# Another order of v, q and k and of the weights' combinations, with p1 written into the second group's PSUM bank, in a graph attention kernel

## The chip, the cores and the metric

The kernel runs on one core of one Trainium2 chip. The metric is the device time of one execution in microseconds (us). All runs of this study on one core were in the fast state, with a mean granted TensorE clock of 0.991 to 0.997; where a median is quoted, it is that of three or four executions of a kernel, with their range. The profile is of one such execution.

## The reference, cut to what matters

Two layers on 32 batches of x (512 nodes by 512 features), with one adjacency matrix for all:

```python
# layer 0: a graph convolution, a residual, a layer norm
mi = einsum('bkd,od->bko', x, Wi);  mj = einsum('bkd,od->bko', x, Wj)
x = layernorm(x + deg * (mi + b) + einsum('ij,bjo->bio', a, mj))
# layer 1: attention of 8 heads under the mask adj, a projection, a residual, a layer norm
q, k, v = x @ Wq.T + bq, x @ Wk.T + bk, x @ Wv.T + bv
x = layernorm(x + softmax(mask(q k^T / 8)) v @ Wo.T + bo)
```

## The kernel before

Each 512x512 product with a weight matrix runs in fp32 on TensorE. It is cut into quarters and done with seven quarter products instead of eight, which land in PSUM, TensorE's output memory. They are numbered: product 1 alone is p1, and p1 belongs to all four quarters of the result; products 1 and 2 make the first quarter; 6, 7 and 4 accumulate in one PSUM bank ("the second group" below), which is read out after each of them, with p1 added, into one of the other three quarters; 5 and 3 accumulate in a third group, without p1, and are added to two of these quarters. I write v2 for v's product 2, and so on. The left factors' combinations are made per batch by GpSimd (`combos`), the weights' once at the start (`combine`), and are then fetched from DRAM through a ring of 12 tiles in the order in which TensorE uses them.

There are two PSUM banks for products, "a" and "b". v and k use "a", q uses "b", and one bank can take its next product only when the last has been read out ("evacuated"). This is the evacuation before:

```python
        if i == 1:
            p1 = OPEN[kind, b, "p1"] = work([P, 2, Q], "p1", 3)
            nc.scalar.copy(p1, pm)
        ...
        if kind in ("l0", "pj"):              # layer 0 and the projection: into y = x
            if i == 1:
                for n, f in ((1, 0), (1, 1), (0, 1)):
                    d = quarter(y, n, f)
                    nc.gpsimd.tensor_tensor(d, d, p1, op=OP.add)
            else:
                nc.vector.tensor_tensor(d, d, pm, op=OP.add)
        elif kind == "v":
            if i == 2:                     nc.scalar.copy(d, pm)
            elif i in (6, 7, 4):           nc.vector.tensor_tensor(d, pm, p1, op=OP.add)
            elif i != 1:                   nc.vector.tensor_tensor(d, d, pm, op=OP.add)
        ...                                  # q and k likewise, with their biases
```

A period handles one batch through v, q and k, while the attention steps of the batch before and the projection of the one before that are laid between the products. The list for one batch n (m = n - 2); `apply` is the layer norm's last step, on ScalarE, `l0_norm` a transpose for v, q, k, `ahead` the split of the next x into two parts for the gather, `z` a piece without TensorE work. Further words used below: the gathers are the adjacency matrix times x on TensorE, the base step is x + deg * b on VectorE, oT is the attention's output from which the projection is made, and the fold takes the bias of v through Wo, once:

```python
        res += [norm[0], norm[1], z(apply, n, 1), pc("v", n, 1, "a"), pc("q", n, 1, "b")]
        ...
        res += [norm[2], norm[3], z(combos, TH, n, h, (1, 2)), pc("v", n, 2, "a"), pc("q", n, 2, "b"),
                pc("k", n, 1, "a"), z(combos, TH, n, h, (3, 4)), z(add_bo, n, 0), z(add_bo, n, 1), pc("k", n, 2, "a")]
        if m >= 0:
            res += [z(apply, m, 0), z(apply, m, 1), z(store, m)]
        for i in ORDER[2:]:                       # 6, 7, 4, 5, 3
            res += [pc("v", n, i, "a"), pc("q", n, i, "b")]
            if i == 5 and n + 1 < B and n > 0:
                res += [z(load_x, n + 1)]
        if n + 1 < B:
            res += [z(ahead, n + 1)]
        # then, in phase_a(n + 1): k's products 6, 7, 4, 5, 3 (bank "a") with the gathers of batch n + 1
```

Of the kernel before, what the change touches and what calls it, by code (L numbers as in the profile page):

```python
# [25 lines left out]
def gnn_attention_kernel(  # L26
# [101 lines left out]
    load_x(0)  # L128
    ident = const.tile([P, P], FT, name="ident")
# [5 lines left out]
    W = {}  # L135
    W["wj"] = load_w(big(), wjT, nc.sync)
    W["wi"] = load_w(big(), wiT, nc.sync)
    W["wv"] = load_w(work([P, NC, D], "v", 2), wvT, nc.sync)
    W["wq"] = load_w(work([P, NC, D], "v", 2), wqT, nc.sync)
# [20 lines left out]
    W["wk"] = load_w(big(), wkT, nc.sync)  # L160
    W["wo"] = load_w(wo, woT, nc.sync)
    load_x(1)
# [28 lines left out]
    ahead(0)  # L191

# [3 lines left out]
    def graph_forms():  # L196
        nc.vector.tensor_tensor(adj_f, adjT, adjR.bitcast(FT), op=OP.not_equal)
        nc.vector.reduce_sum(told[:, B * HP:], adj_f.rearrange("p c i -> p (c i)"), axis=AX.X)
        nc.vector.tensor_scalar(told[:, B * HP:], told[:, B * HP:], 2.0 * SAFE, None, op0=OP.mult)
        nc.vector.tensor_scalar(edge, adjT, 0.0, None, op0=OP.not_equal)  # L200
# [8 lines left out]
    def combine(name, eng):  # L209

        w = W[name]
        a11, a12, a21, a22 = [w[:, 2 * j:2 * j + 2, Q * i:Q * i + Q] for i in range(2) for j in range(2)]
        s1, s2, s3, s4, n22 = [t[:, c].rearrange("p (c i) -> p c i", c=2)
                               for t in [work([P, 2, N], "e", 4) for _ in range(3)] for c in range(2)][:5]
        eng.tensor_tensor(s1, a21, a22, op=OP.add)
        eng.tensor_tensor(s2, s1, a11, op=OP.subtract)
        eng.tensor_tensor(s4, a12, s2, op=OP.subtract)
        eng.tensor_tensor(s3, a11, a21, op=OP.subtract)
        nc.scalar.mul(n22, a22, -1.0)
        for i, t in ((6, s2), (7, s3), (4, n22), (5, s1), (3, s4)):  # L220
            WS[name, i] = dram.tile([P, 2, Q], FT, name=f"{name}_{i}")
            nc.sync.dma_start(WS[name, i], t)
# [8 lines left out]
    def prefetch():  # L231
        while len(TILES) < min(len(KEYS), ring.used + RING):
            t = ring_tile()
            nc.sync.dma_start(t, WS[KEYS[len(TILES)]])
            TILES.append(t)
# [103 lines left out]

    def piece(kind, b, i, bank):  # L340
        g = GROUP[i]
        first = (kind, b, g) not in OPEN
        if first:
            OPEN[kind, b, g] = mm_tile(bank)
        pm = OPEN[kind, b, g]
        terms = []
        for name, (quarters, T) in zip(NAMES[kind], sources(kind, b)):
            a = {1: (0, 0), 2: (1, 0), 3: (1, 1)}.get(i)
            terms.append((take((name, i)), quarters(*a) if a else T[:, {5: 0, 6: 1, 7: 2, 4: 3}[i]]))
        for c in range(2):  # L350
            for n, (w, t) in enumerate(terms):
                for kc in range(2):
                    cut = slice(c * P, (c + 1) * P)
                    lhs, rhs = (w[:, kc, cut], t[:, kc, :]) if kind in "qk" else (t[:, kc, cut], w[:, kc, :])

                    nc.tensor.matmul(pm[:, c * Q:(c + 1) * Q], lhs, rhs, start=first,  # L356
                                     stop=(kc == 1 and n == len(terms) - 1), skip_group_check=True)
                    first = False
        prefetch()
        pm = pm.rearrange("p (c i) -> p c i", c=2)  # L360
        if i == 1:
            p1 = OPEN[kind, b, "p1"] = work([P, 2, Q], "p1", 3)
            nc.scalar.copy(p1, pm)  # L363
        p1 = OPEN[kind, b, "p1"]
        f, n = {1: (0, 0), 2: (0, 0), 6: (0, 1), 3: (0, 1), 4: (1, 0), 7: (1, 1), 5: (1, 1)}[i]
        if kind in ("l0", "pj"):
            y = XT[b]
            if i == 1:
                for n, f in ((1, 0), (1, 1), (0, 1)):
                    d = quarter(y, n, f)  # L370
                    nc.gpsimd.tensor_tensor(d, d, p1, op=OP.add)  # L371
            else:
                d = quarter(y, n, f)
                nc.vector.tensor_tensor(d, d, pm, op=OP.add)  # L374
        elif kind == "v":
            if i == 1:
                V[b] = work([P, NC, D], "v", 2)
            d = quarter(V[b], n, f)
            if i == 2:
                nc.scalar.copy(d, pm)  # L380
            elif i in (6, 7, 4):
                nc.vector.tensor_tensor(d, pm, p1, op=OP.add)
            elif i != 1:
                nc.vector.tensor_tensor(d, d, pm, op=OP.add)
        else:
            T, bias = (QT, bq_c) if kind == "q" else (KT, bk_c)
            if i != 1 and (b, f) not in T:
                T[b, f] = work([P, 2, N], kind, 3)
            if i in (6, 7):
                nc.vector.tensor_tensor(T[b, f][:, :, Q * n:Q * n + Q], pm, p1, op=OP.add)  # L390
            elif i != 1:
                for c in range(2):
                    d = T[b, f][:, c, Q * n:Q * n + Q]
                    bc = bias[:, 2 * f + c:2 * f + c + 1]
                    if i == 2:
                        nc.scalar.activation(d, pm[:, c, :], AF.Identity, bias=bc, scale=1.0)
                    else:
                        o = p1[:, c, :] if i == 4 else d
                        nc.vector.scalar_tensor_tensor(d, pm[:, c, :], bc, o, op0=OP.add, op1=OP.add)
# [75 lines left out]
    def phase_a(n):  # L475

        g = [(TR + GA, l0_gather, n, dc) for dc in range(DC)] if n < B else []
        k = [pc("k", n - 1, i, "a") for i in ORDER[2:]] if n > 0 else []
        res = []
        for i in range(max(len(g), len(k))):  # L480
            res += k[i:i + 1] + g[i:i + 1]
            if n == 0 and i == 3:
                res += [z(graph_forms)]
            if i == (3 if n == 0 else 1) and g:
                res += [z(combos, TX, n, lambda j, m: quarter(XD[n], j, m), (1,)),
                        z(combos, TA, n, lambda j, m: quarter(AX_T[n], j, m), (1,))]
        if g:
            res += [z(combos, TX, n, lambda j, m: quarter(XD[n], j, m), (2,)),
                    z(combos, TA, n, lambda j, m: quarter(AX_T[n], j, m), (2,)),
                    z(base, n, 0),  # L490
                    z(combos, TX, n, lambda j, m: quarter(XD[n], j, m), (3, 4)),
                    z(combos, TA, n, lambda j, m: quarter(AX_T[n], j, m), (3, 4)),
                    z(base, n, 1)]
        return res
# [10 lines left out]
    def phase_b(n):  # L505

        m = n - 2
        if m < 0:
            res = []
            for i, bank in ALONE:  # L510
                if n == 0:
                    res += [z(combine, *f) for f in {6: (("wv", nc.vector),), 2: (("wq", nc.vector),),
                                                     5: (("wk", nc.vector),)}.get(i, ())]
                res.append(pc("l0", n, i, bank))
                if i == 4:
                    res += [z(stats, n, 0)]
            return res + [z(apply, n, 0), z(stats, n, 1)]
        res = []
        for i in ORDER:
# [8 lines left out]
            if i == 4:  # L528
                res.append(z(apply, n, 0))
        return res  # L530

    def phase_c(n):
# [4 lines left out]
        res = [z(fold)] if n == 0 else []  # L537
        res += [norm[0], norm[1], z(apply, n, 1), pc("v", n, 1, "a"), pc("q", n, 1, "b")]
        if m >= 0:
            res += [z(stats, m, 1)]  # L540
        res += [norm[2], norm[3], z(combos, TH, n, h, (1, 2)), pc("v", n, 2, "a"), pc("q", n, 2, "b"),
                pc("k", n, 1, "a"), z(combos, TH, n, h, (3, 4)), z(add_bo, n, 0), z(add_bo, n, 1), pc("k", n, 2, "a")]
        if m >= 0:
            res += [z(apply, m, 0), z(apply, m, 1), z(store, m)]
        for i in ORDER[2:]:
            res += [pc("v", n, i, "a"), pc("q", n, i, "b")]
            if i == 5 and n + 1 < B and n > 0:
                res += [z(load_x, n + 1)]
# [4 lines left out]
    def fold():  # L553

        combine("wo", nc.vector)
        pd = mm_tile("b")
        bv_w = work([P, DC, P], "big", 6)
        for dc in range(DC):
            nc.vector.tensor_scalar(bv_w[:, dc, :], ones, bv_c[:, dc:dc + 1], None, op0=OP.mult)
            nc.tensor.matmul(pd, bv_w[:, dc, :], W["wo"][:, dc, :], start=(dc == 0), stop=(dc == DC - 1))  # L560
# [12 lines left out]
    def last_steps():  # L573
# [5 lines left out]
        return [[z(last_load), p[0], FLUSH] + c, [p[1], p[2]], [p[3], p[4]], [p[5], p[6], z(stats, m, 0), z(stats, m, 1)],  # L579
# [8 lines left out]
    def last_load():  # L588
        W["wo"] = load_w(work([P, NC, D], "xh", 3), woT, nc.sync)

    def last_part(hp, half):
# [6 lines left out]
        for ic in range(2 * half, 2 * half + 2):  # L598
            nc.tensor.matmul(ACC[ic], OT[B - 1, hp // 2][:, hp % 2, ic * P:(ic + 1) * P], W["wo"][:, hp, :],
# [28 lines left out]
    combine("wj", nc.gpsimd)  # L628
    combine("wi", nc.vector)
    prefetch()  # L630

    for f in PERIODS[0]:
        run(f)
# [181 lines left out]
```

## Time and profile before

The time was 4021.6 us (4021.29 to 4022.62). A period is the distance between two equal instructions of neighbouring batches.

| what | value | view |
|---|---|---|
| one period, of 29 undisturbed ones | 122.53 us | chain of waits |
| TensorE busy in it | 120.15 us | stretches |
| VectorE, GpSimd, ScalarE busy in it | 80.4, 57.8, 32.9 us | stretches |
| from the start to the first attention scores | 143.20 us | TensorE's timeline |
| from the start to the base step of batch 2 | 252.91 us | chain of waits |
| from the last base step to the end | 215.24 us | chain of waits |

The waits view of TensorE sums what stood before its instructions over the whole execution: engine and line, what was waited for and where that was made, then us in total, times, and the longest.

```profile
PE mma L356 <- issue: 29.3, 30, 1.0
PE mma L356 <- ACT p L363: 20.9, 31, 0.7
PE mmb L280 <- ACT big L286: 14.8, 2, 14.5
PE mma L356 <- DVE v L382: 9.4, 29, 0.3
PE mmb L356 <- POOL big L325: 8.0, 2, 4.9
```

Entries with 29 to 31 times are per-period waits; entries with one or two belong to the start and the end. L356 is the matmul of all quarter products (L380 in the changed kernel), L363 the copy of p1 (L387).

### The profile page before, as it was taken

The page shows a single profiled execution, that of the slowest core. Times are in us where ns is not written, and L with a number is a line of the kernel's source. Part 1 is how long each engine was busy: PE and PEld are TensorE (multiplying, and loading weights), DVE is VectorE, ACT ScalarE, POOL GpSimd, SP SyncE. Part 2 cuts the span into 40 slices and gives each one's busy share as a digit, 9 for nine tenths or more (in the row PEclk, how much of TensorE's full clock was granted, in tenths as well). Part 3 has the DMA queues.
Part 4 walks back from the last instruction along what each step waited for, and adds up shares of the span by engine and source line. Part 5 has one row for each costly group of instructions (what it writes and reads, how often), then busy time and mean ns, then how long its engine had stood idle before and what let it go on. Part 6 is the DMA issues. An engine that isn't in the chain of part 4 may idle for free.

```text
span 4021.7 us, 47158 instructions
## 1 busy us (share of the span) xinstructions
PE 3876.8 (96%) x17418; PEld 2655.3 (66%) x17418; DVE 2608.9 (65%) x3524; ACT 1059.7 (26%) x1483; POOL 1851.6 (46%) x1866
## 2 busy tenths in 40 slices
PE   6999999999999999999999999999999999999997
PEld 4766666666666666666666666666666666666663
DVE  4466666666666666666666666666666666676666
ACT  1212222222222223222222222232222222222222
POOL 3445445445345454454453454444444534544432
PEclk8999999999999999999999999999999999999998
DMA  7333343333333333333333333333333334333330
GB/s 251 103 99 106 108 121 100 103 108 110 110 115 92 113 108 103 122 100 103 108 113 108 118 89 112 109 107 116 105 98 113 107 110 118 95 106 112 105 107 22
DMA packets 284346, 437.55 MB, mean 109 GB/s; under 512 B 23248, under 2 KB 121040, under 8 KB 284112
## 3 DMA queue, kind: packets, MB, share of 16 engines
q1 hardware_dynamic: 283856, 433.94, 35.9%
q8 instruction: 142, 2.33, 0.2%
q0 software_dynamic: 256, 0.53, 0.1%
q14 instruction: 92, 0.75, 0.1%
HBM read 392.96 MB, written 41.42 MB: 108 GB/s over the span
## 4 chain that ended last, share of the span: by engine, by line
PE 81%; DVE 14%; issue 3%; ACT 1%; POOL 1%; DMA 0%; SPq 0%; POOLq 0%; ACTq 0%; DVEq 0%
PE mma L356 32%; PE mmb L356 17%; PE sc L408 10%; PE ov L430 10%; PE mmb L280 6%; DVE xh L293 5%; DVE rl L443 3%; PE ov L437 2%; DVE es L422 2%; DVE e L413 2%; PE sc L273 1%; PE sc L301 1%; DVE ov L448 1%; ACT big L302 0%; ACT p L363 0%
## 5 line engine op out<-in xcount | busy, mean ns | idle before, releaser
L356 PE MATMUL mma<-ring,big 128*128 128x256 f32 x5288 | 1228.1, 382 | 47.3 <-issue 29.3
L356 PEld LDWEIGHTS mma<-ring,big 128*128 128x128 f32 x5288 | 991.6, 190 | 236.4 <-issue 66.3
L412 ACT ACTIVATE sc<-sc 128x1024 f32<-128x1024 f32 x512 | 492.8, 1006 | 1563.2 <-PE sc L408 1562.1
L413 DVE TENSOR_TENSOR e<-sc,edge 128x1024 f32<-128x1024 f32 x512 | 602.4, 1217 | 355.9 <-ACT sc L412 355.9
L419 POOL TENSOR_TENSOR es<-e 128x1024 f32<-128x1024 f32 x128 | 301.0, 2352 | 778.4 <-PE ov L437 778.4
L325 POOL TENSOR_TENSOR big<-big 128x512 f32<-128x512 f32 x384 | 525.0, 1390 | 236.5 <-DVE big L274 196.8
L408 PE MATMUL sc<-q,k 64*128 64x512 f32 x2048 | 509.7, 616 | 0.2 <-ACT big L302 0.2
L430 PE MATMUL ov<-e,v 128*64 128x512 f32 x2048 | 497.5, 607 | 6.5 <-DVE told L448 6.5
L443 DVE RECIPROCAL rl<-ov 128x128 f32<-128x128 f32 x512 | 458.7, 927 | 5.4 <-PE ov L437 1.6
L356 PE MATMUL mma<-big,ring 128*128 128x256 f32 x1792 | 430.2, 383 | 24.6 <-ACT p L363 20.9
L248 POOL TENSOR_SCALAR mv<-mv 128x1 f32<-128x1 f32 x256 | 79.2, 309 | 774.6 <-DVE mv L247 759.8
L356 PE MATMUL mmb<-big,ring 128*128 128x256 f32 x1792 | 432.6, 384 | 0.0
L356 PEld LDWEIGHTS mmb<-big,ring 128*128 128x128 f32 x1792 | 333.1, 190 | 113.9 <-issue 47.9
L356 PEld LDWEIGHTS mma<-big,ring 128*128 128x128 f32 x1792 | 334.8, 190 | 110.5 <-ACT p L363 33.4
L430 PEld LDWEIGHTS ov<-e,v 128*64 128x64 f32 x2048 | 124.7, 136 | 347.5 <-issue 272.8
L422 DVE TENSOR_TENSOR es<-es,e 128x1024 f32<-128x1024 f32 x256 | 313.5, 1225 | 4.4
L408 PEld LDWEIGHTS sc<-q,k 64*128 64x128 f32 x2048 | 176.5, 186 | 209.4 <-issue 195.8
L371 POOL TENSOR_TENSOR xh<-xh,p 128x512 f32<-128x512 f32 x189 | 235.5, 1274 | 104.5 <-ACT p L363 103.8
L374 DVE TENSOR_TENSOR xh<-xh,mma 128x512 f32<-128x512 f32 x189 | 127.8, 676 | 232.4 <-PE mma L356 232.4
L356 PE MATMUL mmb<-ring,big 128*128 128x256 f32 x1080 | 267.3, 392 | 10.7 <-POOL big L325 8.0
L183 POOL TENSOR_TENSOR xlo<-xh,xhi 128x512 fp32r<-128x512 f32 x128 | 162.6, 1281 | 220.8 <-ACT xhi L182 220.7
L356 PEld LDWEIGHTS mmb<-ring,big 128*128 128x128 f32 x1080 | 203.9, 194 | 90.7 <-POOL big L325 33.1
(109 smaller groups left out, 3667.0 us busy)
## 6 DMA issues: line engine op xcount, KB each, us to landing
ring<-wi SPq DMA_DIRECT2D x160, 256.0 KB, 2.6
ring<-wj SPq DMA_DIRECT2D x160, 256.0 KB, 2.8
ring<-wv SPq DMA_DIRECT2D x160, 256.0 KB, 2.7
ring<-wq SPq DMA_DIRECT2D x160, 256.0 KB, 2.7
ring<-wk SPq DMA_DIRECT2D x160, 256.0 KB, 4.4
ring<-wo SPq DMA_DIRECT2D x155, 256.0 KB, 2.6
xh<-in_x_dram SPq DMA_DIRECT2D x32, 1024.0 KB, 5.5
out_dram<-xh SPq DMA_DIRECT2D x31, 1024.0 KB, 5.1
```

The source lines that it names most:

```text
L280: nc.tensor.matmul(pm, parts[w][:, jc, :], adjR[:, jc, :], start=(w == 0 and jc == 0), stop=(w == 1 and jc == NC - 1))
L293: nc.vector.scalar_tensor_tensor(y, b0_r, deg_c[:, ic:ic + 1], y, op0=OP.mult, op1=OP.add)
L325: nc.gpsimd.tensor_tensor(dst, p, q, op=OP.subtract)
L356: nc.tensor.matmul(pm[:, c * Q:(c + 1) * Q], lhs, rhs, start=first, stop=(kc == 1 and n == len(terms) - 1), skip_group_check=True)
L371: nc.gpsimd.tensor_tensor(d, d, p1, op=OP.add)
L408: nc.tensor.matmul(ps[:, s, :], KT[b, hp // 2][r, hp % 2, kc * P:(kc + 1) * P], QT[b, hp // 2][r, hp % 2, :], start=True, stop=True)
L412: nc.scalar.activation(ps, ps, AF.Exp, scale=QSCALE)
L413: nc.vector.tensor_tensor(e, ps, edge[:, kc:kc + 1, :].to_broadcast([P, 2, N]), op=OP.mult)
L419: nc.gpsimd.tensor_add(ES[hp], E[0], E[1])
L422: nc.vector.tensor_add(ES[hp], ES[hp], E[kc])
L430: nc.tensor.matmul(PV[hp][s * HD:(s + 1) * HD, :], V[b][:, kc, c0:c0 + HD], E[kc][:, s, :], start=(kc == 0), stop=(kc == NC - 1))
L443: nc.vector.reciprocal(rl[:, c], pl[:, c])
```

## The change

Its intent: p1 is no longer added three times by GpSimd or VectorE. ScalarE copies it into the bank of the second group (a "seed"), products 6, 7 and 4 accumulate on top of it without clearing, and ScalarE can evacuate products 6, 7 and 4 of v, q and k with a plain copy or bias. A new order of v, q and k is to give each bank's evacuation another product to hide behind. At the start, the weights' combinations come in two parts, placed between the gathers, and the weights are loaded from ScalarE's queue.

```diff
+    def seed(kind, b, bank):
+        pm = OPEN[kind, b, "Y"] = mm_tile(bank)
+        nc.scalar.copy(pm.rearrange("p (c i) -> p c i", c=2), OPEN[kind, b, "p1"])
 ...
-        if first:
+        if first and g == "Y":
+            seed(kind, b, bank)
+            first = False
+        elif first:
             OPEN[kind, b, g] = mm_tile(bank)
 ...
+        new = i in (2, 6, 7, 4)
         if kind in ("l0", "pj"):
-            if i == 1:
-                for n, f in ((1, 0), (1, 1), (0, 1)):
-                    d = quarter(y, n, f)
-                    nc.gpsimd.tensor_tensor(d, d, p1, op=OP.add)
 ...
+        if i == 2 and (kind == "q" or kind == "l0" and b >= 2 or kind == "pj" and b < B - 2):
+            seed(kind, b, bank)
 ...
-        res += [norm[2], norm[3], z(combos, TH, n, h, (1, 2)), pc("v", n, 2, "a"), pc("q", n, 2, "b"),
-                pc("k", n, 1, "a"), z(combos, TH, n, h, (3, 4)), z(add_bo, n, 0), z(add_bo, n, 1), pc("k", n, 2, "a")]
+        res += [pc("v", n, 2, "a"), norm[2], norm[3], z(combos, TH, n, h, (1, 2)), pc("k", n, 1, "a"),
+                z(combos, TH, n, h, (3, 4)), pc("q", n, 2, "b"), pc("k", n, 2, "a"), z(seed, "v", n, "a")]
 ...
-            res += [pc("v", n, i, "a"), pc("q", n, i, "b")]
+            res += [pc("q", n, i, "b"), pc("v", n, i, "a")]
 ...                                       # the start
-    combine("wj", nc.gpsimd)
-    combine("wi", nc.vector)
-    prefetch()
+            # now in parts, inside phase_a(0): wj on GpSimd (part 1 behind all combos), wi on VectorE;
+            # load_x(1) and prefetch() only in front of the first product of layer 0;
+            # fold (bias of v through wo) no longer ahead of v but at the end of phase_a(1)
```

Cut: the second half of the evacuation (q, k, v), the parts of `combine` and `graph_forms`, the moved `add_bo`, and the renaming of weight halves.

## The prediction

> **What bounds the kernel now.** I read the page's busy shares first, then the stretches view over whole periods, then TensorE's and ScalarE's timelines inside one period. The page:
>
> ```profile
> PE 3876.8 (96%) x17418; PEld 2655.3 (66%) x17418; DVE 2608.9 (65%) x3524; ACT 1059.7 (26%) x1483; POOL 1851.6 (46%) x1866
> PE   6999999999999999999999999999999999999997
> PEclk8999999999999999999999999999999999999998
> ```
>
> TensorE is full but for the first and last fortieth, at full clock. The chain view repeats the base step (L293) every 122.53 us (1110.63, 1233.16, ...), one period per batch. The stretches view, columns span, PE, PEld, DVE, ACT, POOL, clock, DMA share, GB/s:
>
> ```profile
> 0.00:175.00 175.00, 135.95 (x566) 102.95 (x567) 82.61 (x100) 32.43 (x52) 70.43 (x68) 0.90 0.57 191
> 1110.63:1233.16 122.53, 120.15 (x548) 82.65 (x546) 80.43 (x111) 32.87 (x46) 57.77 (x59) 1.00 0.36 108
> 2090.90:2213.43 122.53, 120.15 (x548) 82.65 (x546) 80.42 (x110) 32.87 (x46) 57.78 (x59) 1.00 0.37 108
> ```
>
> A period has 120.15 us of matmuls and only 2.38 idle; the start has 39 us idle in 175. So the change can win in two places: the few waits of a period, times about 30, and once in the start. Work taken from VectorE (80 of 122 us) and GpSimd (58) is worth nothing by itself. TensorE's timeline names the waits of one period:
>
> ```profile
> 1180.54 1.99 PE L356 MATMUL mma<-big,ring 128*128 128x256 f32 x8 [0.68 <-ACT p L363]
> 1183.51 1.97 PE L356 MATMUL mma<-ring,big 128*128 128x256 f32 x8 [0.97 <-issue]
> 1198.41 1.99 PE L356 MATMUL mma<-ring,big 128*128 128x256 f32 x8 [0.32 <-DVE v L382]
> ```
>
> The reader should see that all are bank "a" waiting for its own evacuation: k's product 2 for the copy of p1, v's product 6 for k's evacuation, and a later v. The idle entry understates them, because the modelled end of a matmul overlaps the next. From starts: an undisturbed product of v, q or k takes 1.73 us (1185.31 to 1187.03). k1 started at 1177.97, k2 at 1180.54: 0.84 lost. v6 at 1183.51: 1.24 lost. The last, 1196.20 to 1198.41: 0.48 lost. With 0.43 at the projection that waits for oT and 0.41 after a transpose, a period loses 3.4 us. That is all that a perfect new order could win, 2.8%.
>
> **What the Trainium skill says.** "Perfetto Trace Analysis", Matmuls, says that independent matmul groups should rotate through PSUM banks so that an evacuation overlaps the next group's matmuls. The waits above agree: each sits where two neighbours share bank "a". "PSUM — Partial Sum Buffer", The four PSUM rules, says that ScalarE's writes do not set the bits that decide whether a matmul accumulates, so a written seed is kept only where an earlier matmul left the bit set. Here each seeded bank was written in full by a product or a gather before; I expect right results, and no trace yet shows it. "TensorE: Matmul & The Clock Gate", Part 1, gives a half-rate clock after an idle window of about 3.4 us. The start agrees: after a wait of 14.55 us eight gather matmuls took 2.07 us, later 1.20.
>
> **The change, part by part, in a period.**
>
> Removed: 6 GpSimd additions of p1 to x (L371, 1.27 us each, 7.6 us), and VectorE's p1 additions for v, q, k. Products 6, 7, 4 are now evacuated by ScalarE. Added on ScalarE: five seeds, p1 copied into the bank (like L363's 585 ns: 2.9 us), three v copies (1.76) and six evacuations in pairs (0.84 a pair at 1178.17: 5.0), some 9.7 us. ScalarE goes from 32.9 to about 42.6 us of 122.5. None of it is a bound by busy time; what matters is the order in which ScalarE, an in-order engine, reaches it.
>
> The built order on TensorE is now: v2 right after q1; two transposes; k1(a), q2(b), k2(a), q6(b), v6(a), q7(b), scores, values, v7, q4, v4, q5, v5, q3, scores, values, sums, v3(a), k6(a).
>
> Gain 1: between k1 and k2 stands q2, 1.73 us, and p1's copy needs 0.2 to start and 0.58: the 0.84 goes. Between k2 and v6 stands q6: k2's evacuation (0.2+0.84) and v's seed (0.58) take 1.62, just under 1.73: the 1.24 goes nearly whole.
>
> Loss 1, q7. ScalarE's built order there is: k2's pair, v's seed, **four layer norm applications of the older batch**, q6's pair, v6's copy. Before, the four stood in the same place, but q6 and v6 were then evacuated by VectorE:
>
> ```profile
> 1182.57 0.84 ACT L396 ACTIVATE k<-mma,bk_c 128x256 f32<-128x256 f32 x2 [2.08 <-PE mma L356]
> 1183.30 2.92 ACT L253 ACTIVATE xh<-xh,mv 128x512 f32<-128x512 f32 x4
> ```
>
> Four applications take 2.92 us and already had their inputs when ScalarE reached them. Count from k2's end: pair done at 1.04, seed 1.65, applications 4.6, q6's pair 5.45, q7 may start at 5.55. Without the wait it would start after q6 and v6, at 3.45. **Loss 2.1 us**, so the stretch k1 to q7 gives back what it won (0.84+1.24 = 2.08).
>
> Loss 2, k6. Swapping v and q puts v3(a) right in front of k6(a), and k is not seeded early. Before, q3(b) and an attention step stood between them. Now k6 waits for v3's addition on VectorE (0.2 to start, 0.69), then the seed (0.07, 0.58), then the weight load (0.1 to 0.2): **loss 1.7 us**.
>
> Gain 2: the 0.48 at the late v goes, because ScalarE is free there. Gain 3: k3's addition takes 0.69 instead of a 0.88 pair, which brings the oT chain forward by 0.1 to 0.2.
>
> Seeds that I expect hidden: q's (q2's pair and seed take 1.62 beside k2's 1.73), the projection's (scores or a layer 0 product beside it), and layer 0's (VectorE freed the bank at 1124.33, +0.07+0.58 = 1124.98, and product 6 started at 1125.19 anyway).
>
> Sum per period: -0.84 -1.24 -0.48 -0.1 +2.1 +1.7 = **+1.1 us**; over 30 periods **+34 us**.
>
> **The start.** Before, the combinations' output tiles ran out and blocked ScalarE and with it the second gather:
>
> ```profile
> 36.63 2.07 PE L280 MATMUL mmb<-adjR,xhi 128*128 128x512 f32 x4 [14.55 <-ACT big L286]
> 52.66 6.61 PE L356 MATMUL mmb<-ring,big 128*128 128x256 f32 x16 [3.02 <-POOL big L325]
> 86.69 6.64 PE L560 MATMUL mmb<-xh,big 128*128 128x512 f32 x8 [5.51 <-DVE big L559]
> ```
>
> The change takes that copy off ScalarE and places combinations between gathers, so gathers should end near 28 instead of 46. But the layer 0 tiles are now fetched behind the stores of wj's second part, which GpSimd makes after eight combos of 1.27 us: near 40, plus the issue, x(1)'s 1 MB ahead in the queue and 2.7 us to land: layer 0 starts at 43 to 46, no gain. Its seven products (3.45 each) ran from 46.0 to 81.2, 35 us for 24; with the combos done beforehand I expect some 29, two waits of 0.9 (product 2 on p1's copy, 7 on 6) and a cold start included. Gain 6. The bias fold (L560, about 6.6 us cold with a 5.5 wait) leaves the gap between layer 0 and v and returns later at some 3.5 us; that gap was 13.3 (81.2 to 94.5), and should be some 3.5 (stats, GpSimd chain and apply still have to run): gain 10, minus 3.5 for the fold. From v1 on little else. Sum of the start **-13 to -15**.
>
> The end: the last projection waited 4.94 us for GpSimd combos behind p1 additions (3.7 us) that are gone: -3. The last k products all stand in bank "a", and ScalarE's pair is slower than VectorE's addition: +1. Sum **-2**.
>
> Total: 4021.6 + 34 - 14 - 2 = 4040 us.
>
> **Rivals.** (1) The intended gain: every period wait but transpose and oT goes, ScalarE's order does no harm; 2.56 x 30 = 77 us off, with the start 3930. For it: ScalarE is busy only 26%. Against it: q7's wait on ScalarE stands in the built program, and the applications are ahead of it there. It would need ScalarE to reach q6's pair at once; I see no way. Between the two lies a case in which one of my two losses is smaller than I count. (2) ScalarE's queue becomes worse than counted: seeds also delay the exps, scores wait for their tiles, and each period loses 2 to 3 us: 4070 to 4100. For it: ten more operations in a row, several awaited within 1.7 us. Against it: values use the exps of the step before, an attention step's slack. (3) VectorE or GpSimd as the hidden bound, relieved by 8 to 10%: 4000. Against it: in a period TensorE idles 2.38 us only, and only oT's wait hangs on VectorE's length. (4) The start is hidden or worse, because the weights now queue behind adj on ScalarE's queue: +10.
>
> **Range and chances.** The two losses are sums of durations in the trace; an error of 0.8 us per period in either direction is 24 us, the start is good to 8 us. So 4012 to 4066 for 8 in 10. Two per cent faster is below 3941 and needs rival 1 nearly whole: 0.03. Two per cent slower is above 4102, rival 2 at its worst: 0.03. Within 2%: 0.94.
>
> **What would show it.** In the changed profile: a period of about 123.6 us; TensorE's wait at q7 of 1.7 to 2.1 us, released by ScalarE with four applications just before it; a wait of 1.4 to 1.7 at k6, released by the seed; none left at k2 and v6; GpSimd near 50 us and ScalarE near 42 a period; the first scores near 129 instead of 143.20. I am wrong if the period is below 122.5, which means that one of the two losses is not there, or if waits stand at exps or scores.

## The result, and the profile after

The changed kernel took **4077.28 us** (4075.09 to 4078.05), beside 4022.11 us (4021.29 to 4023.55) for the kernel before in the same rounds: a ratio of 1.0136, 95% interval 1.0118 to 1.0153. Ratios here are the mean of one kernel's runs over that of the other's of the same rounds, so not quite the ratio of the medians. The result is correct. It is slower by 1.4%, and 11 us above the upper end of the predicted range.

TensorE's busy tenths are the same digits as before. First the page's busy times, then the stretches view over one period (columns: span, PE, PEld, DVE, ACT, POOL, clock, DMA share, GB/s):

```profile
PE 3872.5 (95%) x17418; PEld 2647.3 (65%) x17418; DVE 2401.4 (59%) x3049; ACT 1364.5 (33%) x2116; POOL 1628.1 (40%) x1678
```

```profile
1133.08:1257.38 124.30, 120.15 (x546) 82.50 (x546) 74.07 (x95) 42.53 (x66) 50.53 (x53) 1.00 0.35 106
```

ScalarE (42.5) and GpSimd (50.5) are where they were predicted, and TensorE's busy time in a period is the same 120.15 us; only the period has grown, by 1.77 us. So the loss is all waiting. From the chain of waits the difference splits into three parts:

| part | before | after | difference | predicted |
|---|---|---|---|---|
| start, to the base step of batch 2 | 252.91 | 262.96 | +10.1 | -14 |
| 29 periods, 122.53 and 124.30 each | 3553.6 | 3604.7 | +51.2 | +34 (for 30) |
| tail | 215.24 | 207.8 | -7.4 | -2 |
| span of the profiled execution | 4021.7 | 4075.5 | +53.8 | +18 |

TensorE's waits view after shows two new entries with 31 times and a new one of 23 us that came once. The entry for p1's copy is as large as before (21.2 beside 20.9 us), but it now stands at another product, v2 instead of k2:

```profile
PE mmb L380 <- issue: 49.3, 31, 1.6
PE mma L380 <- ACT mma L359: 47.9, 31, 4.2
PE mma L380 <- DMA ring<-in_wiT_dram: 23.3, 1, 23.3
PE mma L380 <- ACT p L387: 21.2, 31, 0.7
PE mmb L588 <- DVE big L587: 7.4, 1, 7.4
```

And TensorE's timeline of the period from 1133.08, cut to the three products with a wait of over 0.5 us (v2, q7, k6):

```profile
1192.29 1.99 PE L380 MATMUL mma<-ring,big 128*128 128x256 f32 x8 [0.68 <-ACT p L387]
...
1210.31 1.97 PE L380 MATMUL mmb<-big,ring 128*128 128x256 f32 x8 [1.61 <-issue]
...
1234.64 1.99 PE L380 MATMUL mma<-big,ring 128*128 128x256 f32 x8 [1.46 <-ACT mma L359]
```

The idle entry in brackets understates a wait, so I count from starts, with 1.73 us for an undisturbed product. q1 started at 1189.71 and v2 at 1192.29: 0.85 lost. v6 at 1206.80, q7 at 1210.31: 1.78 lost. v3 at 1231.19, k6 at 1234.64: 1.72 lost. With 0.43 at the projection that waits for oT and 0.41 behind a transpose, as before, that is 5.19 us a period, against 3.40 before. The difference of 1.79 is the growth of the period (1.77). None of the waits at k2, v6 and the late v is left.

**q7 and k6** came as predicted. ScalarE's timeline around q7, then VectorE's and ScalarE's around k6:

```profile
1206.04 0.59 ACT L359 COPY mma<-p 128x512 f32<-128x512 f32 x1
1206.57 2.92 ACT L269 ACTIVATE xh<-xh,mv 128x512 f32<-128x512 f32 x4
1209.39 0.81 ACT L409 ACTIVATE q<-mmb,bq_c 128x256 f32<-128x256 f32 x2
```

```profile
1233.22 0.69 DVE L401 TENSOR_TENSOR v<-v,mma 128x512 f32<-128x512 f32 x1 [2.10 <-PE mma L380]
1234.00 0.59 ACT L359 COPY mma<-p 128x512 f32<-128x512 f32 x1 [2.06 <-DVE v L401]
```

Four applications of the older batch (2.92 us) stand in front of q6's evacuation at 1209.39, and q7 starts when that ends. At k6, the addition and the seed have nothing beside them.

**v2** was not predicted at all. ScalarE's timeline just before it, after the change and then before it:

```profile
1190.95 0.81 ACT L269 ACTIVATE xh<-xh,mv 128x512 f32<-128x512 f32 x1 [1.92 <-POOL mv L266]
1191.67 0.56 ACT L387 COPY p<-mma 128x512 f32<-128x512 f32 x1
```

```profile
1168.23 0.81 ACT L253 ACTIVATE xh<-xh,mv 128x512 f32<-128x512 f32 x1 [1.92 <-POOL mv L250]
1168.95 0.57 ACT L363 COPY p<-mma 128x512 f32<-128x512 f32 x1
```

The picture is the same in both: p1's copy stands behind the newer batch's application, which waits for GpSimd's statistics. But before, two transposes lay between q1 and v2, as TensorE's timeline of the kernel before shows:

```profile
1167.00 1.89 PE L356 MATMUL mmb<-big,ring 128*128 128x256 f32 x8
1168.73 1.04 PE L301 MATMUL sc<-ident,xh 128*128 128x128 f32 x8
1169.60 1.97 PE L356 MATMUL mma<-ring,big 128*128 128x256 f32 x8
```

There p1's copy ended at 1169.52, and v2 began at 1169.60 without a wait: from q1's start to v2's it was 2.60 us, of which the transposes filled 0.87. Now it is 2.58, v2 comes directly behind q1, and 0.85 of it is idle. The delay was always there; the change took away what TensorE did meanwhile. The Trainium skill ("Perfetto Trace Analysis", Per-engine timelines, Tensor Engine Instruction (MATMUL, LD_WEIGHTS)) says that ScalarE, VectorE and GpSimd are "strict FIFO"; these lines agree, because TensorE had left v1 by 1189.71, where q1 starts, while v1's copy began at 1191.67, behind an application with 1.92 us of idle time in front of it.

**The start.** The timeline of the first 60 us, cut to VectorE's base step, GpSimd's combos, the DMA queue (SPq) and TensorE's first product of layer 0; then the fold:

```profile
34.95 5.75 DVE L309 SCALAR_TENSOR_TENSOR xh<-b_r,deg_c,xh 128x512 f32<-128x512 f32 x4
35.18 11.13 POOL L341 TENSOR_TENSOR big<-big 128x512 f32<-128x512 f32 x6 [1.78 <-DVE big L290]
47.56 0.91 SPq L238 DMA_DIRECT2D wj<-e  x2
49.03 0.57 SPq L250 DMA_DIRECT2D ring<-in_wiT_dram  x1
55.08 6.11 PE L380 MATMUL mma<-ring,big 128*128 128x256 f32 x16 [23.33 <-DMA ring<-in_wiT_dram]
```

```profile
138.62 6.43 DVE L309 SCALAR_TENSOR_TENSOR xh<-b_r,deg_c,xh 128x512 f32<-128x512 f32 x4
145.40 5.31 PE L588 MATMUL mmb<-xh,big 128*128 128x512 f32 x8 [7.42 <-DVE big L587]
```

Layer 0 starts at 55.08 instead of 46.02, because the ring's first tile is issued behind the stores of wj's second part, and that part behind GpSimd's combos. Six of these took 11.13 us, 1.85 us each. I had counted with 1.27. VectorE's base step and further two-input operations ran beside them. The trace of the kernel before already had this: at its start seven combos took 11.83 us, 1.69 each, and in a usual period of both kernels the three combos beside the base step take 1.71 to 1.74 us each, the other twelve 1.25 to 1.29. The Trainium skill ("GPSIMD Engine Reference", 1. Specifications) says that GpSimd shares its SBUF interfaces with VectorE and names contention with VectorE's instructions with two SBUF inputs; these times agree with that, though no run here changed that alone. The long combos, 3.5 us more than at 1.27, are one part of the delay: the gathers ended at 31.75 instead of the predicted 28, GpSimd waited 1.78 us for VectorE in front of the six, and the ring's first tile took 6.01 us from its issue to landing, beside 2.7 in the prediction.

The fold, the other piece, now stands behind batch 1's base step (6.43 us), waits 7.42 us, and then takes 5.31 us at a granted clock of 0.68; e7 below shows it at 3.70 without the wait, at a clock of 1.00. Afterwards the first scores start at 150.64 instead of 143.20. The second period has a further 4.24 us at k6: k's seed stands behind the split of the next x on ScalarE, which waits for x's load. That load takes 5.57 us, as usual, but the attention step that otherwise lies between its issue and k6 is missing there. e9 and e11 test this queue.

### The profile page after: what moved, and what is told of

It is laid out like the page before. It is cut to its first block, busy times and chain, and to the rows that moved or that the text cites. A ratio compares the mean times of both kernels' runs of the same rounds, so it can differ in the third digit from the quotient of the medians.

```text
span 4075.5 us, 46994 instructions
## 1 busy us (share of the span) xinstructions
PE 3872.5 (95%) x17418; PEld 2647.3 (65%) x17418; DVE 2401.4 (59%) x3049; ACT 1364.5 (33%) x2116; POOL 1628.1 (40%) x1678
## 4 chain that ended last, share of the span: by engine, by line
PE 77%; DVE 15%; POOL 3%; ACT 2%; issue 2%; DMA 1%; SPq 0%; ACTq 0%; POOLq 0%; DVEq 0%
PE mma L380 32%; PE mmb L380 16%; PE sc L423 10%; PE ov L445 9%; PE mmb L296 6%; DVE xh L309 5%; DVE e L428 3%; DVE rl L458 3%; PE ov L452 2%; PE sc L289 1%; POOL mv L265 1%; DVE st L262 1%; POOL mv L264 1%; PE sc L317 1%; ACT sc L427 1%
## 5 line engine op out<-in xcount | busy, mean ns | idle before, releaser
L458 DVE RECIPROCAL rl<-ov 128x128 f32<-128x128 f32 x512 | 446.4, 917 | 5.7 <-PE ov L452 1.9
L437 DVE TENSOR_TENSOR es<-es,e 128x1024 f32<-128x1024 f32 x256 | 325.9, 1273 | 4.4
L269 ACT ACTIVATE xh<-xh,mv 128x512 f32<-128x512 f32 x256 | 198.6, 809 | 236.6 <-POOL mv L266 221.1
```

The costliest lines, as they stand in the source:

```text
L269: nc.scalar.activation(y, y, AF.Identity, bias=mv[:, 4:5], scale=mv[:, 3:4])
L437: nc.vector.tensor_add(ES[hp], ES[hp], E[kc])
L458: nc.vector.reciprocal(rl[:, c], pl[:, c])
```

## The experiments

**Theory.** In a period, three operations stand at the wrong place of an in-order queue: the older batch's applications before q6's evacuation (q7), the newer batch's application before p1's copy (v2), and v3 directly before k6. The start has two such places, the ring behind wj's second part and the fold behind the base step. Seeding itself is cheap. **Rival A:** seeding and evacuating on ScalarE is the cost, wherever things stand. **Rival B:** the new order is the cost. All kernels gave correct results and were timed in three rounds.

| run | what | median us (range) | ratio to before (95%) | usual period |
|---|---|---|---|---|
| after | the change | 4077.28 (4075.09 to 4078.05) | 1.0136 (1.0118 to 1.0153) | 124.30 |
| e1 | new order, old evacuation | 4024.35 (4023.53 to 4025.83) | 1.0006 (0.9990 to 1.0023) | 122.44 |
| e9 | old order, seeds | 4038.76 (4034.34 to 4041.00) | 1.0038 (1.0021 to 1.0055) | 122.57 |
| e11 | e9, x loaded earlier | 4026.62 (4022.98 to 4027.42) | 1.0010 (0.9993 to 1.0027) | 122.57 |
| e2 | older applications moved | 4022.38 (4020.52 to 4023.81) | 1.0002 (0.9985 to 1.0018) | 122.45 |
| e3 | p1's copies first | 4050.03 (4049.18 to 4051.14) | 1.0070 (1.0053 to 1.0086) | 123.35 |
| e4 | gather between v3 and k6 | 4028.52 (4027.13 to 4030.28) | 1.0015 (0.9998 to 1.0032) | 122.59 |
| e5 | e2, e3, e4 | 3946.18 (3943.04 to 3947.98) | 0.9812 (0.9796 to 0.9828) | 119.79 |
| e10 | e5 with the old evacuation | 3971.00 (3969.31 to 3974.24) | 0.9873 (0.9857 to 0.9890) | 120.45 |
| e6 | ring and wj early | 4058.64 (4057.10 to 4063.81) | 1.0091 (1.0075 to 1.0108) | 124.31 |
| e7 | fold ahead of base | 4071.61 (4069.35 to 4072.83) | 1.0123 (1.0106 to 1.0140) | 124.31 |
| e8 | e5, e6, e7 | 3918.63 (3917.07 to 3921.64) | 0.9745 (0.9729 to 0.9762) | 119.79 |

### e1: the new order with the old evacuation

The evacuation of the kernel before, p1 added by GpSimd and VectorE, in the changed kernel's order:

```diff
-        if first and g == "Y":
-            seed(kind, b, bank)
-            first = False
-        elif first:
+        if first:
 ...          # and the branches for l0, pj, v, q, k as in the kernel before
-                ... pc("k", n, 2, "a"), z(seed, "v", n, "a")]
+                ... pc("k", n, 2, "a")]
```

> The new order alone: the changed kernel with p1 added by GpSimd and VectorE as in the kernel before, no seeds. My theory (the seeds put ScalarE's queue and a longer chain in front of TensorE, the order alone costs only v2's and k6's wait): the 1.6 us wait at q7 goes, k6's wait shrinks from 1.46 to about 0.9 (VectorE's addition without the seed behind it), v2's 0.68 stays; period 121.8 to 122.3 us, time 4003 to 4015. Rival (the new order is what costs, and the seeds earn something back): period over 124.3, time over 4077.

Measured: 4024.35 us, a little above the 4003 to 4015 expected, and a period of 122.44. TensorE's timeline has v2's wait (0.68) as in the changed kernel, and these two, at a q product and at k6:

```profile
1201.87 1.99 PE L372 MATMUL mmb<-big,ring 128*128 128x256 f32 x8 [0.51 <-DVE q L415]
1214.67 1.99 PE L372 MATMUL mma<-big,ring 128*128 128x256 f32 x8 [0.78 <-DVE v L400]
```

I had not expected the first: a q product waits for VectorE, which still evacuates q here. So the new order alone costs nothing in a usual period (122.44 against 122.53), but it doesn't bring much either. Rival B falls.

### e9: the old order with the seeds

```diff
-        res += [pc("v", n, 2, "a"), norm[2], norm[3], z(combos, TH, n, h, (1, 2)), pc("k", n, 1, "a"),
-                z(combos, TH, n, h, (3, 4)), pc("q", n, 2, "b"), pc("k", n, 2, "a"), z(seed, "v", n, "a")]
+        res += [norm[2], norm[3], z(combos, TH, n, h, (1, 2)), pc("v", n, 2, "a"), pc("q", n, 2, "b"),
+                pc("k", n, 1, "a"), z(combos, TH, n, h, (3, 4)), pc("k", n, 2, "a"), z(seed, "v", n, "a")]
 ...
-            res += [pc("q", n, i, "b"), pc("v", n, i, "a")]
+            res += [pc("v", n, i, "a"), pc("q", n, i, "b")]
```

> The fourth corner: the changed kernel with v, q and k in the order of the kernel before, seeds and ScalarE evacuations kept. My theory (seeds cost only where the new order leaves nothing beside them): k2's and v6's waits of before are back, v6's grown by the seed to about 1.9 us, q7's, k6's and v2's waits are gone; period about 122.7 us, time about 4030. Rival (the seeds cost 1.9 us per period in any order, because ScalarE is the engine that is late): period about 124.4, time about 4080.

Measured: 4038.76 us, between the two, with a usual period of 122.57. So in a usual period **seeding costs nothing in the old order, the new order costs nothing without seeds, and the two together cost 1.8 us.** (The kernel before also has `add_bo` in another place, so this corner differs by that too.) Rival A falls too, as a cost of seeding by itself. TensorE waits here at k2 and at v6, as before the change:

```profile
1074.74 1.99 PE L380 MATMUL mma<-big,ring 128*128 128x256 f32 x8 [0.68 <-ACT p L387]
1078.33 1.97 PE L380 MATMUL mma<-ring,big 128*128 128x256 f32 x8 [1.60 <-issue]
```

The late v's wait is gone and v6's has grown from 0.97 to 1.60 by v's seed, so that the balance is zero. But five of the 29 periods were longer, by 0.8 to 4.4 us, 9.9 us in all. In the longest, the chain of waits has a load of x, and ScalarE's and TensorE's timeline shows how it reaches k6:

```profile
1341.98 8.60 DMA xh<-in_x_dram
```

```profile
1350.61 1.14 ACT L185 CAST xhi<-xh 128x512 fp32r<-128x512 f32 x2 [4.36 <-DMA xh<-in_x_dram]
1351.65 0.58 ACT L359 COPY mma<-p 128x512 f32<-128x512 f32 x1
1352.29 3.22 PE L380 MATMUL mma<-big,ring 128*128 128x256 f32 x8 [2.50 <-ACT mma L359]
```

k's seed stands behind the split of the next x in ScalarE's queue. The median load of x takes 5.6 us and fits; one of 8.6 does not. Without seeds, k6 needed nothing from ScalarE there. The 4.24 us in the changed kernel's second period come from the same queue, though with a load of usual length.

### e11: e9 with the load of x issued earlier

```diff
-            if i == 5 and n + 1 < B:
+            if i == 7 and n + 1 < B:
                 res += [z(load_x, n + 1)] if n > 0 else []
```

> e9 (old order of v, q, k with p1's copies kept) has an undisturbed period of 122.57 us, but five of 29 periods were 0.8 to 4.4 us longer, 9.8 us in all, each with a load of x of 6.7 to 8.6 us in the chain that ended last, ahead of ScalarE's cast of x and, behind it in the same queue, k's seed. Here the issue of that load is moved two pairs of products earlier (behind product 7 instead of product 5 of v and q), some 5 us. Theory (the late x, felt by the seed behind the cast): the long periods go, and so does the 4 us wait in the second period: 122.57 throughout, about 4025 us. Rival (the long loads stretch with when they are issued, or something else lengthens those periods): 4034 to 4040 us as in e9.

Measured: 4026.62 us. All 29 periods are 122.57 to 122.59, and the second one is 121.16 instead of 129.12. That shows the cause of e9's long periods.

### e2, e3, e4: one misplaced operation each

e2 puts the older batch's applications and its store right behind v2, where ScalarE has time:

```diff
-        res += [pc("v", n, 2, "a"), norm[2], norm[3], z(combos, TH, n, h, (1, 2)), pc("k", n, 1, "a"),
+        res += [pc("v", n, 2, "a")]
+        if m >= 0:
+            res += [z(apply, m, 0), z(apply, m, 1), z(store, m)]
+        res += [norm[2], norm[3], z(combos, TH, n, h, (1, 2)), pc("k", n, 1, "a"),
 ...
-        if m >= 0:
-            res += [z(apply, m, 0), z(apply, m, 1), z(store, m)]
```

> The changed kernel with the four layer norm applications of the older batch moved from behind v's seed to in front of the third and fourth transpose. My theory (q7's wait is ScalarE's order, nothing else): that wait goes, 1.78 us per period, 30 periods: period 122.5, time about 4024. Rival (ScalarE has too much to do between k2 and q7 with the seeds): the wait is only moved, period over 123.5, time over 4055.

Measured: 4022.38 us and 122.45 a period, 1.85 less than the change; the wait at q7 is gone, those at v2 and k6 stand.

e3 puts the newer batch's application behind p1's copies:

```diff
-        res = [norm[0], norm[1], z(apply, n, 1), pc("v", n, 1, "a"), pc("q", n, 1, "b")]
+        res = [norm[0], norm[1], pc("v", n, 1, "a"), pc("q", n, 1, "b"), z(apply, n, 1)]
```

> The changed kernel with the newer batch's second half of layer norm applications issued behind the copies of p1 of v and q. My theory (v2's wait of 0.68 is not the copy, which takes 0.56, but the application ahead of it that waits for GpSimd's statistics): the wait goes, 0.85 us per period: period 123.45, time about 4051. Rival (the copy is simply too near, one product of 1.73 us is not enough): unchanged, 4077.

Measured: 4050.03 us and 123.35 a period, 0.95 less; only the wait at v2 is gone. This is the wait that the prediction had missed.

e4 seeds k directly behind v3 and lays the first gather of the next batch between v3 and k6; the split of x moves ahead of v3, so that the gather has its input:

```diff
-            res += k[i:i + 1] + g[i:i + 1]
+            res += ([z(seed, "k", n - 1, "a"), g[0], k[0]], [g[1], k[1]], [k[2], g[2]], [k[3], g[3]], [k[4]])[i] if g and k else ...
 ...
-            res += [pc("q", n, i, "b"), pc("v", n, i, "a")]
+            res += [pc("q", n, i, "b")]
+            if i == 3 and n + 1 < B:
+                res += [z(ahead, n + 1)]
+            res += [pc("v", n, i, "a")]
```

> The changed kernel with the next batch's first gather between v3 and k6, k's seed issued ahead of it, and x's split issued ahead of v3. My theory (k6 waits for v3's addition and the seed behind it, 1.72 us, because nothing stands between): the wait goes: period 122.6, time about 4022. Rival (it waits for x's load, which holds ScalarE's queue): the wait turns up at the gather instead, period above 123.8, time above 4060.

Measured: 122.59 a period, 1.71 less, as expected; but 4028.52 us, 6 more than expected. Four periods with loads of x of 6.4 to 7.1 us are longer, by 1.1 us in all: the split of x is now reached earlier, so the load has less room. The tail is 3.0 us longer than the changed kernel's. The rest is in the first two periods, where a gather waits 2.45 us for x's load and two k products wait 0.93 each.

### e5 and e10: all three together, with and without the seeds

e5 has the three edits of e2, e3 and e4.

> The three moves of the runs before together (applications of both batches moved, gather in front of k6). My theory (three separate waits of TensorE, none hides another): the gains add, 1.85 + 0.95 + 1.71 us per period: period 119.8, time about 3942, faster than the kernel before by 2.0%. Rival (the engines behind are now late in other places, and a wait taken away comes back elsewhere): period over 121, time over 3980.

Measured: 3946.18 us and 119.79 a period. The three gains add up to the hundredth: 1.85 + 0.95 + 1.71 = 4.51, and 124.30 - 119.79 = 4.51. So the three waits were independent, and no wait took their place. e10 has the same three moves with e1's evacuation:

```diff
-            res += ([z(seed, "k", n - 1, "a"), g[0], k[0]], ...
+            res += ([g[0], k[0]], ...
 ...          # evacuation as in e1, no seed anywhere
```

> Question: does the gain of e5 (3946 us, period 119.79) need p1's copy in the bank, or is it the moved operations alone? This kernel has e5's order and moves (applications and store behind v's product 2, p1's copies ahead of the newer batch's application, the gather between v's product 3 and k's product 6) with the evacuation of the kernel before: p1 added by GpSimd and VectorE, no copy into the bank. Theory (both are needed): e1, which is the new order with the old evacuation, had 122.44 us a period and waits of about 0.85 at v's product 2, 0.7 at a q product behind VectorE, 0.95 at k's product 6. The moves take away the first and the third, the one on VectorE stays: 120.5 to 120.9 us a period, 3966 to 3978 us. Rival (the order alone does it): 119.8, about 3946 us.

Measured: 3971.00 us and 120.45 a period, with the wait for VectorE's q still there, as expected:

```profile
1191.50 1.99 PE L372 MATMUL mmb<-big,ring 128*128 128x256 f32 x8 [0.51 <-DVE q L415]
```

Usual periods, in one table:

| order | p1 added by GpSimd and VectorE | p1 seeded by ScalarE |
|---|---|---|
| old | 122.53 (before) | 122.57 (e9) |
| new | 122.44 (e1) | 124.30 (after) |
| new, three operations moved | 120.45 (e10) | 119.79 (e5) |

In the last row the seeds are worth 0.66 us a period and 25 us in the whole; the same seeds cost 1.86 a period in the row above. About two thirds of e5's gain over the kernel before come from the new order and the moves, without seeds. "Seeded" stands here for two things, p1's copy into the bank and ScalarE's evacuation of products 6, 7 and 4 of v, q and k, and no run separates them. The starts in e1's and the changed kernel's timelines do say where the 1.86 are: q7's 1.78 belongs to the evacuation, while at k6 the seed makes 1.72 out of 1.05, as much as is saved at the q product that waits for VectorE (0.67).

### e6 and e7: the start

e6 makes wj's second part right behind the first and fills the ring before the gathers:

```diff
-                res += [z(combine, "wj", nc.gpsimd, 0)]
+                res += [z(combine, "wj", nc.gpsimd, 0), z(combine, "wj", nc.gpsimd, 1)]
 ...
+    prefetch()
     for i, f in enumerate(PERIODS[0]):
```

> The changed kernel with the first four layer 0 weight tiles fetched ahead of the combinations' stores, and wj's second part of combinations made right behind its first. My theory (layer 0 starts at 55 us because its tiles stand in the queue behind stores that wait for GpSimd): it starts near 33 us, and the time falls by 15 to 20 us, to about 4059. Rival (GpSimd's combos of x would hold layer 0's third product back anyway): starts early but waits there, gain under 8 us.

Measured: 4058.64 us. Layer 0 starts 21.4 us earlier, and 18.6 us of that reach the end; the third product gives some back:

```profile
33.69 4.87 PE L380 MATMUL mma<-ring,big 128*128 128x256 f32 x16
...
46.32 5.38 PE L380 MATMUL mmb<-ring,big 128*128 128x256 f32 x16 [3.36 <-DMA ring<-wi]
```

e7 puts the fold in front of the base step (and its small operand into a buffer of p1, because the kernel deadlocks there with the old one; no such run is on record):

```diff
+            if n == 1 and i == 2:
+                res += [z(fold)]
 ...
-        if n == 1:
-            res += [z(fold)]
 ...
-        bv_w = work([P, DC, P], "big", 6)
+        bv_w = work([P, 2, Q], "p1", 3).rearrange("p c (d i) -> p (c d) i", i=P)
```

> The changed kernel with the bias fold put between two gathers of batch 1, ahead of layer 0's base on VectorE (its tile from another buffer tag, since the old one deadlocks there). My theory (the fold waits 7.42 us for the base's four operations and then runs on a cold clock): a gain of 7 to 9 us, time about 4069. Rival (the wait was hidden behind combos that the first layer 0 product needs anyway): no gain.

Measured: 4071.61 us, 5.7 less than the change; I had expected 7 to 9. The base step of batch 2 does start 8.7 us earlier (254.27 instead of 262.96). Of these, two longer periods take back 0.8, and the tail is 3.2 us longer: its waits are the same, but the granted clock between 70 and 25 us before the end was 0.85, against 0.92 in the changed kernel. The first scores start at 141.19 instead of 150.64. The fold itself, behind a wait of only 0.68:

```profile
131.80 3.70 PE L588 MATMUL mmb<-xh,p 128*128 128x512 f32 x8 [0.68 <-ACT big L302]
```

### e8: everything

All five edits of e2, e3, e4, e6 and e7.

> All five moves together. My theory: the gains add: 3942 less 18 less 8, about 3916, period 119.8, faster than the kernel before by 2.6%. Rival: as for the three moves and the start, over 3960.

Measured: 3918.63 us, **2.55% faster than the kernel before** and 159 us faster than the change. In a usual period two short waits are left, behind the transpose and at oT:

```profile
1009.75 1.99 PE L380 MATMUL mma<-ring,big 128*128 128x256 f32 x8 [0.24 <-ACT big L318]
...
1088.16 1.56 PE L380 MATMUL mmb<-ring,oT 128*128 128x256 f32 x6 [0.17 <-DVE oT L468]
```

The stretches view over such a period has TensorE busy for 119.39 of 119.79 us: in the steady state little is left to win by order.

## Why the prediction was wrong

The time, 4077, was outside of 4012 to 4066; that it stays within 2% was right. Of the 37 us between 4040 and 4077 (36 in the profiled executions), 17 are in the periods and 24 in the start, and the tail gives 5 back. Either v2's 25 us below or the start's 24 would by itself have left the time inside the range: e3, without v2's wait, took 4050.

**The periods: the list of losses was incomplete.** "Sum per period: +1.1" should have been +1.77.
- Gain 1 (k2 and v6, 2.08) and Gain 2 (the late v, 0.48): right, none of these waits is left.
- Loss 1 (q7, 2.1): right in mechanism, measured 1.78: neighbouring instructions of ScalarE overlap by about 0.1 us (1206.57 begins before 1206.04 + 0.59 is over), and v6 itself came 0.1 later than counted. e2 takes the wait away by moving the four applications.
- Loss 2 (k6, 1.7): right, 1.72. e4 takes it away.
- **The failed step: v2.** The text put v2 "right after q1" and looked no further. In fact 0.85 us a period are lost there, 25 us in all, more than the 17 that the periods' sum was off. p1's copy behind the newer batch's application was in the trace of the kernel before; there two transposes (0.87 us) hid it. I had checked the queue for those evacuations that changed engine (q6, v6) and those that came close together (v3, k6), not for those whose only change was that the next product now follows at once. e3 shows it: one operation moved, and only this wait goes.
- Gain 3 (oT, 0.1 to 0.2): not there; the wait at oT is 0.43 in both.
- Two readings were wrong without harm to the sum: of the three waits of the kernel before, the late v's does not sit between two neighbours of bank "a", because a q product stands between them (1196.20); and the line at 36.63 is of four gather matmuls, not eight.

So 0.85 missed, 0.15 not gained and 0.3 counted too much make the 0.7.

**The start: predicted -14, measured +10.** Its parts by TensorE's timeline:
- "Layer 0 starts at 43 to 46": measured 55.08, **mis-sized terms**. The chain was right (ring behind the stores, stores behind GpSimd's combos), but the gathers ended at 31.75, not near 28, GpSimd then waited 1.78 for VectorE, six combos took 1.85 us each, not 1.27, and the first tile landed after 6.01 us, not 2.7: durations from undisturbed stretches were used for a busy one. e6 shows that the chain is the cause.
- Layer 0 some 29 us instead of 35: measured 28.75, right. The gap to v1, 13.3 to 3.5: measured 4.64, nearly right.
- "The fold returns later at some 3.5 us": **failed**. It cost a wait of 7.42 us and then 5.31, because it stood behind VectorE's base step, an operation of its own batch list that I had not looked at. Such a slow run after a wait I had described for the kernel before; e7 brings 3.70. So the first scores came at 150.64, not near 129.
- "From v1 on little else": 4.24 us of the second period were lost to x's load ahead of k's seed.

**The tail: -2, measured -7.4.** The wait of 4.94 us for GpSimd is gone whole, not by 3, and with it some 2.5 us by which the two products behind it ran slower than elsewhere; I see nothing of the +1. The size is in part luck: over the changed kernel and its seeded variants the tail is anything from 205.1 to 211.0 us.

**The rivals.** Rival 2 (4070 to 4100, ScalarE's queue worse than counted) got the time, but by other operations than it named: no wait stands at exps or scores. Rival 4 (the start worse by 10) got the size by another way; the weights' place on ScalarE's queue is not on the path that I followed. (The chain of waits does name wk's load on that queue, 9.51 us from 19.27, ahead of GpSimd's split of x at 28.79, but GpSimd was at work almost without a pause from 23.25 until then. No run moved these loads.) Rival 1 named the right amount of idle time and the right condition, "ScalarE reaches q6's pair at once"; e2 meets it by moving four instructions. I had seen "no way" because I looked at the change as it stood only.

The range was too narrow for what it rested on: an error of "0.8 us a period in either direction" covers one forgotten wait, and the start was held "good to 8 us" on a chain of five steps.

## What to carry to other kernels

When an order of work changes, go through every bank in the new order and ask for each evacuation what stands in front of it in its engine's queue, and what it waits for, also where neither the evacuation nor its engine was changed: a delay that a neighbour used to hide becomes a wait. Two edits that cost nothing alone in a usual period can cost 1.8 us a period together, so test them in a table of two by two before one is blamed; and before such a change is given up, try moving the few operations that the waits name, which here turned 1.4% slower into 2.5% faster. Take durations for a sum from a stretch in which the same neighbours are busy.

## What the Trainium skill lacked or had wrong

- "PSUM — Partial Sum Buffer", Summary: rules for kernel authors, says that a sum seeded by VectorE or ScalarE must start from 0 on trn2. Stricter than what ran here: the change and all nine seeded variants of it accumulate on a non-zero p1 copied in by ScalarE and gave correct results. The page's own four rules allow it, on a condition that the summary leaves out: in this program the bank has been written in full by an earlier matmul, and the products on top are issued without clearing.
- "Perfetto Trace Analysis", Matmuls, advises to rotate banks so that an evacuation overlaps the next group's matmuls. What it lacks is the queue of the evacuating engine: q7 stood in another bank than its neighbour v6, and still lost 1.78 us, because 2.92 us of other work stood ahead of q6's evacuation.
- None has it, as far as I found: how far the time of one and the same load spreads. Here a 1 MB load of x took 5.6 us in the median and up to 8.6 in e9's periods, and the long ones cost e9 9.9 us.
